# Compressed entries from projected tokens: one 257-column projection, a softmax in 32x32 turned blocks, and x loaded twice

## The chip, the core and the metric

The kernel runs on one NeuronCore of a Trainium2 chip. The metric is device time in microseconds; the time before is the median of three runs, 2910.0 us (2906.97 to 2914.53). All work is in float32 unless said otherwise. A core has a matrix engine (TensorE, PE in the profile, with PEld for its weight loads), three engines for elementwise work (VectorE = DVE, ScalarE = ACT, GpSimd = POOL), and SyncE (SP), whose queue issues most transfers here. A float32 matrix product appears in the trace as two passes, so a product over four blocks of the inner dimension gives eight.

## The reference, cut to what matters

```python
xn = layernorm(x)                                   # x: (4, 1024, 512)
# one compressed entry for every 4 tokens
w_cmp   = softmax((xn @ Wcmp + bcmp).reshape(B, 256, 4))
entries = einsum('bcr,bcrh->bch', w_cmp, xn.reshape(B, 256, 4, 512))
ck = rope(rmsnorm(entries @ Wk + bk, kn_w), block_ends)
cv = entries @ Wv + bv
# 16 heads of 128: the 8 best entries of each query, and a local window of 128
q  = rope(rmsnorm(heads(xn @ Wq + bq), qn_w))
lk = rope(rmsnorm(heads(xn @ Wlk + blk), kn_w));  lv = heads(xn @ Wlv + blv)
merged = 0.5 * (top8_attention(q, ck, cv) + window_attention(q, lk, lv))
out = x + merged @ Wo + bo + fp8_rounded(xn) @ fp8_rounded(input2)
```

The change concerns the lines from `w_cmp` to `cv`, and where `x` comes from in the last line.

## The kernel before, in words

The 4 x 1024 tokens are 32 chunks of 128 tokens, `t = 0..31`, eight chunks to a batch row, `c = t % 8`. A chunk has eight units `u = 0..7` of two heads each, so there are 256 units. One loop over `s = -2..257` writes all engines' programs in order by hand; each engine then runs its own instructions strictly in that order, waiting on semaphores. At step `s` it issues, among others: the scores of unit `s` (`scores`, L532), the context of unit `s - 2`, the top-8 and softmax work of unit `s` (`weigh`, `settle`), the projections of queries and keys of unit `s + 2` (`queries`, L432: eight passes L437 and one bias product L438), the output product of unit `s - 2` (`to_output`, L700: four passes L707), the turning of the probabilities (`turn`, `fetch`: VectorE transposes 32x32 blocks, SyncE stores them to DRAM as `pr` and reads them back as `probT`), the local values of unit `s + 1` (`values_of`, eight passes L506), normalization and rotation of unit `s + 2`, and its transposed keys, again through DRAM (`turn_keys`, `fetch_keys`: `qk` stored, `qT` and `lkT` read).

Work that is done once a chunk stands in two generators that the loop advances twice in every step, by its two calls of `steps()`: a first half A, between `queries` and `to_output`, and a second half B, between `to_output` and `turn`. `yield "A3"` closes the first half of the generator's fourth step, and so on.

- `chunk_prep(t + 2)` is started at unit 6 of chunk `t`. It normalizes the chunk (A0 to A1), transposes it on TensorE (`xp`, A2) to `xnT`, computes the logits as one row on one partition (`lp`, A3: `Wcmp` columns stationary, `xnT` moving), takes the softmax over groups of four on that row (B3 and A4), spreads the weights over 128 partitions by a product with ones (`wp`, A5), multiplies `xnT` by them and sums fours on VectorE (`prod`, `entT`, B5), projects the 32 entries to `ck` and `cv` (`ep`, A6, with the bias as a bfloat16 product), copies both out of PSUM on ScalarE, normalizes and rotates `ck`, and transposes it into `ckT` (`cp`, A9 and B9). It takes ten steps, the last at unit 7 of chunk `t + 1`.
- `chunk_eight(t)`, started at unit 3, rounds the chunk to fp8, multiplies by `input2` (`fp`), and adds the result to the loaded `x` tile, the residual. `to_output` of unit 7 adds the attention's output and stores the tile.

The PSUM tiles of the generators and of `values_of` come from one ring of two (`pp`); the larger VectorE scratch tiles from a ring of three (`scratch`). `x` tiles come from a ring of three. In the first two steps, `s = -2` and `-1`, `until(first, ...)` drives the generator of chunk 0 ahead, while chunk 1's runs at the normal pace from `s = -2` on. The weights of the first three units are loaded on SyncE's queue before the loop, later ones on ScalarE's queue inside it.

Of the kernel before, what the change touches and what calls it, by code (L numbers as in the profile page):

```python
# [12 lines left out]
F32 = mybir.dt.float32  # L13
BF16 = mybir.dt.bfloat16
# [24 lines left out]
def kernel(  # L39
# [57 lines left out]
    def load_x(t):  # L97
        b, c = divmod(t, NCH)
        xt = work.tile([P, HID], F32, tag="x", name=f"x_{t}", bufs=3)
        nc.sync.dma_start(xt, hidden[b, ts(c, P), :])  # L100
        x_tiles[t] = xt
# [17 lines left out]
    def load_wqk(u, engine):  # L119
        for i, w in enumerate((Wq, Wlk)):  # L120
            engine.dma_start(
                wqk_sb[u][:, :, ts(i, 256)], w[:, ts(u, 256)].rearrange("(k p) n -> p k n", p=P)
            )
# [7 lines left out]
    load_x(0)  # L131
    load_wqk(0, nc.sync)
    load_x(1)
    load_angles(0)
    load_wlv(0, nc.sync)
    wkv_sb = const.tile([P, KK, 2 * D], F32, name="wkv_sb")
    nc.sync.dma_start(wkv_sb[:, :, 0:D], Wk.rearrange("(k p) n -> p k n", p=P))
    nc.sync.dma_start(wkv_sb[:, :, D : 2 * D], Wv.rearrange("(k p) n -> p k n", p=P))
    load_wqk(1, nc.sync)
# [8 lines left out]
    wcmp_sb = const.tile([P, KK], F32, name="wcmp_sb")  # L148
    with nc.allow_non_contiguous_dma(reason="512 words once"):
        nc.scalar.dma_start(wcmp_sb, Wcmp.rearrange("(k p) o -> p (k o)", p=P))  # L150
    nc.scalar.dma_start(bias_f[0:NU, 0:256], bq.rearrange("(u n) -> u n", u=NU))
    nc.scalar.dma_start(bias_f[0:NU, 256:512], blk.rearrange("(u n) -> u n", u=NU))
    nc.scalar.dma_start(bias_f[NU : NU + 1, 0:D], bk.partition_broadcast(1))
    nc.scalar.dma_start(bias_f[NU : NU + 1, D : 2 * D], bv.partition_broadcast(1))
# [5 lines left out]
    bcmp_sb = const.tile([1, 1], F32, name="bcmp_sb")  # L160
    nc.scalar.dma_start(bcmp_sb, bcmp.partition_broadcast(1))
# [7 lines left out]
    ones = const.tile([1, P], F32, name="ones")  # L169
    nc.vector.memset(ones, 1.0)  # L170
# [6 lines left out]
    sel = const.tile([P, NU + 1], BF16, name="sel")  # L177
# [4 lines left out]
    def small_constants():  # L182
        nc.vector.tensor_scalar(
            norm_w[:, 0, :], norm_w[:, 0, :], 1.0 / math.sqrt(D), None, ALU.mult
        )

        part = work.tile([P, 1024], F32, tag="probB", name="part", bufs=1).bitcast(BF16)
        part = part[0:BLK, 0:512]
        nc.vector.tensor_copy(bias_b[0:BLK, :], bias_f)
        nc.vector.tensor_tensor(bias_f, bias_f, bias_b[0:BLK, :], ALU.subtract)  # L190
        nc.vector.tensor_copy(part, bias_f)
        nc.vector.tensor_copy(bias_b[BLK : 2 * BLK, :], part)
        nc.vector.tensor_tensor(bias_f, bias_f, part, ALU.subtract)
        nc.vector.tensor_copy(bias_b[2 * BLK : 3 * BLK, :], bias_f)

        nc.vector.tensor_tensor(
            sel, ident[:, 0 : NU + 1], ident[:, BLK : BLK + NU + 1], ALU.add
        )
        nc.vector.tensor_tensor(
            sel, sel, ident[:, 2 * BLK : 2 * BLK + NU + 1], ALU.add  # L200
        )

# [92 lines left out]
    def chunk_prep(t):  # L295

        b, c = divmod(t, NCH)
        xt = x_tiles[t]
# [28 lines left out]
        lp = pp(f"lp_{t}")  # L327
        for k in range(KK):
            nc.tensor.matmul(  # L329
                lp[0:1, 0:P],  # L330
                wcmp_sb[:, k : k + 1],
                xnT[:, k, :],
                start=(k == 0),
                stop=(k == KK - 1),
            )
        yield "A3"
        wlf = work.tile([P, P], F32, tag="few", name=f"wl_{t}", bufs=1)[0:1, :]
        wl = wlf.rearrange("p (n r) -> p n r", r=RATIO)
        red = work.tile([1, 2, NE], F32, tag="red", name=f"red_{t}", bufs=1)
        nc.vector.tensor_scalar(wlf, lp[0:1, 0:P], bcmp_sb[0:1, 0:1], None, ALU.add)  # L340
        nc.vector.tensor_reduce(red[:, 0, :], wl, AX.X, ALU.max)

        def over_r(v):
            return v.unsqueeze(2).to_broadcast([1, NE, RATIO])

        nc.vector.tensor_tensor(wl, wl, over_r(red[:, 0, :]), ALU.subtract)
        nc.scalar.activation(wlf, wlf, AF.Exp)
        yield "B3"
        nc.vector.tensor_reduce(red[:, 1, :], wl, AX.X, ALU.add)
        nc.vector.reciprocal(red[:, 1, :], red[:, 1, :])  # L350
        nc.vector.tensor_tensor(wl, wl, over_r(red[:, 1, :]), ALU.mult)
        yield "A4"
        yield "B4"
        wp = pp(f"wp_{t}")
        nc.tensor.matmul(wp[:, 0:P], ones, wlf, start=True, stop=True)
        yield "A5"
        prod = scratch(f"prod_{t}", (P, KK, P))
        nc.vector.tensor_tensor(
            prod, xnT, wp[:, 0:P].unsqueeze(1).to_broadcast([P, KK, P]), ALU.mult
        )  # L360
        entT = work.tile([P, KK, NE], F32, tag="entT", name=f"entT_{t}", bufs=1)
        nc.vector.tensor_reduce(
            entT.rearrange("p k n -> p (k n)"),
            prod.rearrange("p k (n r) -> p (k n) r", r=RATIO),
            AX.X,
# [3 lines left out]
        ep = pp(f"ep_{t}")  # L369
        for k in range(KK):  # L370
            nc.tensor.matmul(  # L371
                ep[0:NE, 0 : 2 * D],
                entT[:, k, :],
                wkv_sb[:, k, :],
                start=(k == 0),
                stop=False,
            )
        nc.tensor.matmul(
            ep[0:NE, 0 : 2 * D],
            sel[:, NU : NU + 1].to_broadcast([P, NE]),  # L380
            bias_b[:, 0 : 2 * D],
            start=False,
            stop=True,
        )
        yield "A6"
        yield "B6"
        g, o = divmod(c * NE, P)
        nc.scalar.copy(cv[o : o + NE, g, :], ep[0:NE, D : 2 * D])
        ess = work.tile([NE, 1], F32, tag="ess", name=f"ess_{t}", bufs=1)
        square_sum(ess, ep[0:NE, 0:D], f"e{t}")  # L390
        er = rstd_of(ess, 1, 1.0 / D, EPS_RMS, f"er_{t}")
        ck = work.tile([NE, 1, D], F32, tag="ck", name=f"ck_{t}", bufs=1)
        nc.scalar.copy(ck[:, 0, :], ep[0:NE, 0:D])
        yield "A7"
        yield "B7"
# [3 lines left out]
        ra = work.tile([P, P], F32, tag="few", name=f"ra_e{t}", bufs=1)[0:NE, 0:ROPE]  # L399
        rotate(ck, angles[t][1], 1, ra, f"e{t}")  # L400
        yield "A8"
        yield "B8"
        cp = pp(f"cp_{t}")
        nc.tensor.transpose(cp[:, 0:NE], ck[:, 0, :], ident[:NE, :NE])
        yield "A9"
        nc.vector.tensor_copy(ckT[:, ts(c, NE)], cp[:, 0:NE])
        yield "B9"

    def chunk_eight(t):

        xt, xnT = x_tiles[t], chunks[t]
# [288 lines left out]
    def to_output(n):  # L700
# [13 lines left out]
        if u == NU - 1:  # L714
            xt = x_tiles[t]
            nc.vector.tensor_tensor(xt, xt, op, ALU.add)
            nc.sync.dma_start(out[b, ts(c, P), :], xt)
# [24 lines left out]
    small_constants()  # L742
    until(first, "B3")
    masks()

    for s in range(-2, NN + 2):
        t, u = place(s)

        if u == 6 and t + 2 < NT:
            running = [*running[-2:], chunk_prep(t + 2)]  # L750
        if u == 3 and 0 <= t < NT:
            running = [*running[-2:], chunk_eight(t)]
        if u == 3 and 0 <= t and t + 2 < NT:
            load_x(t + 2)
# [6 lines left out]
        if s < 0:  # L761
            until(first, "B5" if s == -2 else "B7")
# [7 lines left out]
        if s == -1:  # L770
            until(first, "B8")
        for_unit(s + 1, (values_of,))
        if s == -1:
            until(first, "B9")
# [72 lines left out]
```

## Time and profile before

| | |
|---|---|
| median of 3 runs | 2910.0 us (2906.97 to 2914.53) |
| the profiled execution | 2908.4 us, its span 2906.6 us |
| granted TensorE clock, mean | 0.995 |
| lp (L329), 256 passes of 128 columns | 33.9 us busy |
| wp (L355), 64 passes of 128 columns | 15.5 us busy |
| ep (L371), 256 passes of 256 columns, with bias (L378) | 61.2 + 8.7 us busy |
| values (L506), 2048 passes of 256 columns, for comparison | 484.0 us busy |
| prod and its sum on VectorE (L358, L362), 32 each | 21.8 + 21.9 us busy |
| six operations on the one-row logits on VectorE (L340 to L351) | 56.7 us busy |
| x loads on SyncE's queue | 32 of 256 KB, 3.1 us from issue to landing |

"Busy" adds up the time in which an instruction of the group runs on its engine, overlaps counted once. A matmul's recorded end is modelled; consecutive passes overlap in the record, and the distance from one start to the next is what a pass takes of the engine. In the timeline a row gives start, length, engine, line and operation, output from inputs, shape, and how many instructions were merged into it.

### The profile page before, as it was taken

The page shows a single profiled execution, that of the slowest core. Times are in us where ns is not written, and L with a number is a line of the kernel's source. Part 1 is how long each engine was busy: PE and PEld are TensorE (multiplying, and loading weights), DVE is VectorE, ACT ScalarE, POOL GpSimd, SP SyncE. Part 2 cuts the span into 40 slices and gives each one's busy share as a digit, 9 for nine tenths or more (in the row PEclk, how much of TensorE's full clock was granted, in tenths as well). Part 3 has the DMA queues.
Part 4 walks back from the last instruction along what each step waited for, and adds up shares of the span by engine and source line. Part 5 has one row for each costly group of instructions (what it writes and reads, how often), then busy time and mean ns, then how long its engine had stood idle before and what let it go on. Part 6 is the DMA issues. An engine that isn't in the chain of part 4 may idle for free.

```text
span 2906.6 us, 49295 instructions
## 1 busy us (share of the span) xinstructions
PE 2855.3 (98%) x13705; PEld 1899.8 (65%) x13705; DVE 2224.0 (77%) x8636; ACT 1291.5 (44%) x5059; POOL 815.1 (28%) x1126
## 2 busy tenths in 40 slices
PE   5999999999999999999999999999999999999998
PEld 3566666666666666766666666666666666666666
DVE  5777777878777777788877777787887777877776
ACT  2444444444444444444444444444444444444443
POOL 3422222222233222222222332222322323222221
PEclk8999999999999999999999999999999999999999
DMA  8544445554444445454444444554454444455444
GB/s 242 162 129 132 130 134 141 145 146 140 128 115 131 127 130 140 143 144 140 142 126 119 127 130 126 146 148 137 141 143 117 128 124 126 126 146 149 139 142 120
DMA packets 634825, 399.86 MB, mean 138 GB/s; under 512 B 315796, under 2 KB 591030, under 8 KB 634550
## 3 DMA queue, kind: packets, MB, share of 16 engines
q1 hardware_dynamic: 622560, 383.18, 47.2%
q10 hardware_dynamic: 11990, 13.53, 1.5%
q8 instruction: 109, 1.79, 0.3%
q14 instruction: 166, 1.36, 0.2%
HBM read 208.30 MB, written 188.22 MB: 136 GB/s over the span
## 4 chain that ended last, share of the span: by engine, by line
PE 93%; DMA 3%; DVE 1%; SPq 1%; issue 0%; ACT 0%; POOL 0%; ACTq 0%; DVEq 0%; POOLq 0%
PE qp L437 30%; PE op L707 15%; PE vp L506 14%; PE cp L674 13%; PE sc L552 5%; PE sc L549 4%; PE sc L542 4%; PE ep L371 2%; PE qp L438 2%; PE sc L540 2%; DMA lkT<-qk 1%; PE lp L329 1%; PE fp L417 1%; DMA qk<-thb 1%; PE xp L319 0%
## 5 line engine op out<-in xcount | busy, mean ns | idle before, releaser
L437 PE MATMUL qp<-wqk,xnT 128*128 128x512 f32 x2048 | 947.1, 605 | 0.2 <-DMA wqk<-in_L_attn_Wlk_dram 0.2
L437 PEld LDWEIGHTS qp<-wqk,xnT 128*128 128x128 f32 x2048 | 371.3, 191 | 381.2 <-issue 371.0
L579 ACT ACTIVATE prob<-sc,neg 128x256 f32<-128x256 f32 (+1 forms) x512 | 235.6, 460 | 649.8 <-DVE taken L578 639.3
L707 PE MATMUL op<-wo,cT 128*128 128x512 f32 x1024 | 494.4, 605 | 1.0 <-ACT cT L689 1.0
L506 PEld LDWEIGHTS vp<-wlv,xnT 128*128 128x128 f32 x2048 | 388.9, 190 | 161.2 <-issue 103.1
L506 PE MATMUL vp<-wlv,xnT 128*128 128x256 f32 x2048 | 484.0, 379 | 0.0
L623 DVE STREAM_TRANSPOSE probB<-prob 128x512 f32<-128x512 f32 (+2 forms) x510 | 288.7, 603 | 161.1 <-ACT prob L605 157.8
L273 ACT ACTIVATE junk<-qp 128x128 bf16<-128x128 f32 x1024 | 283.6, 277 | 236.5 <-PE qp L438 200.8
L267 POOL TENSOR_SCALAR r<-ss 128x4 f32<-128x4 f32 x256 | 49.8, 194 | 1093.5 <-ACT junk L273 1088.1
L518 ACT COPY lv<-vp 128x256 f32<-128x256 f32 x256 | 95.1, 372 | 537.3 <-PE cp L674 455.1
L286 POOL TENSOR_TENSOR rb<-th,cs 128x256 f32<-128x256 f32 x256 | 247.1, 965 | 286.8 <-DVE th L459 286.8
L459 DVE SCALAR_TENSOR_TENSOR th<-qp,r,norm_w 128x128 f32<-128x128 f32 x1024 | 283.1, 337 | 40.1 <-POOL r L268 40.1
L674 PE MATMUL cp<-probT,lv 128*128 128x128 f32 x1920 | 297.7, 275 | 5.8 <-DMA qk<-thb 3.1
L707 PEld LDWEIGHTS op<-wo,cT 128*128 128x128 f32 x1024 | 181.7, 189 | 174.3 <-issue 96.6
L674 PEld LDWEIGHTS cp<-probT,lv 128*128 128x128 f32 x1920 | 274.8, 191 | 21.1 <-issue 3.6
L268 POOL TENSOR_TENSOR r<-r,nhalf 128x4 f32<-128x4 f32 x256 | 259.7, 1014 | 21.3
L674 PE MATMUL cp<-probT,cv 128*128 128x128 f32 x1536 | 255.2, 275 | 0.0
L574 DVE TENSOR_REDUCE neg<-sc 128x1 f32<-128x256 f32 (+1 forms) x512 | 198.3, 387 | 52.8 <-PE sc L553 52.8
L549 PE MATMUL sc<-lkT,qT 128*128 128x128 f32 x1024 | 210.6, 288 | 27.3 <-DMA lkT<-qk 27.1
L552 PE MATMUL sc<-ckT,qT 128*128 128x96 f32 (+7 forms) x1024 | 226.9, 303 | 0.0
L605 ACT ACTIVATE prob<-prob,tot 128x256 f32<-128x256 f32 (+1 forms) x512 | 222.6, 483 | 3.6 <-DVE tot L599 3.6
L674 PEld LDWEIGHTS cp<-probT,cv 128*128 128x128 f32 x1536 | 212.7, 192 | 0.0
(121 smaller groups left out, 4073.5 us busy)
## 6 DMA issues: line engine op xcount, KB each, us to landing
qk<-thb SPq DMA_DIRECT2D x1024, 64.0 KB, 2.0
pr<-probB SPq DMA_DIRECT2D x127, 512.0 KB, 2.6
probT<-pr SPq DMA_DIRECT2D x508, 128.0 KB, 2.9
pr<-probB SPq DMA_DIRECT2D x96, 384.0 KB, 2.3
probT<-pr SPq DMA_DIRECT2D x384, 96.0 KB, 2.4
qT<-qk SPq DMA_DIRECT2D x256, 128.0 KB, 2.3
lkT<-qk SPq DMA_DIRECT2D x256, 128.0 KB, 2.5
x<-_attn_hidden_states_dram SPq DMA_DIRECT2D x32, 256.0 KB, 3.1
```

The source lines that it names most:

```text
L268: nc.gpsimd.tensor_tensor(r, r, nhalf[: ss.shape[0], 0:n], ALU.pow)
L273: nc.scalar.activation(junk[: src.shape[0]], src, AF.Square, accum_out=acc)
L286: nc.gpsimd.tensor_tensor(bb, x12, wide(cs[:, HALF:ROPE]), ALU.mult)
L437: nc.tensor.matmul(qp, xnT[:, k, :], wqk_sb[u][:, k, :], start=(k == 0), stop=False)
L459: nc.vector.scalar_tensor_tensor(th[:, i, :], qp[:, ts(i, D)], r[:, i : i + 1], norm_w[:, i // 2, :], ALU.mult, ALU.mult,)
L506: nc.tensor.matmul(vp[:, 0:256], xnT[:, k, :], wlv_sb[u][:, k, :], start=(k == 0), stop=(k == KK - 1),)
L549: nc.tensor.matmul(blocks(sc[:, P : 2 * P]), q, lkT[:, :, ds(h * BLK, BLK)], start=False, stop=True)
L552: nc.tensor.matmul(sc[:, spa], q, ckT[:, 0:m], start=True, stop=False)
L579: nc.scalar.activation(prob[:, loc], sc[:, loc], AF.Exp, bias=neg[:, 0:1], accum_out=tot[:, 0:1])
L623: nc.vector.transpose(pb[:, :, ds(h * g, g), :], prob[:, parts[0] * P : (parts[-1] + 1) * P].rearrange("p (g b i) -> p b g i", b=NB, i=BLK),)
L674: nc.tensor.matmul(blocks(cp[:, h, :]), v, probT[:, :, h * len(parts) + i - parts[0], :], start=(i == parts[0]), stop=(i == parts[-1]),)
L707: nc.tensor.matmul(op, cT[:, h, :], wo_sb[u][:, h, :], start=(u == 0 and h == 0), stop=(u == NU - 1 and h == 1),)
```

## The change

The entries are a weighted sum over four tokens and the projection is linear, so the order of the two can be exchanged. After the change the chunk's 128 tokens are projected first, with `Wcmp` as a 257th column beside `Wk` and `Wv`, and the weighted sum of fours is taken over projected tokens by a second product with a 128x32 matrix of unnormalized weights. The normalizing sum comes out of the same product, from a column of ones.

- The logits are now a column over 128 partitions. VectorE turns them in 32x32 blocks into a row of each block (`transpose`), takes maximum and difference over fours there, ScalarE the exponential, and VectorE turns them back.
- `picks`, a 0/1 matrix made once on GpSimd, places each token's weight in its entry's column (`spread_w`).
- The bias is added by VectorE from a broadcast tile after the division by the sum; the bias product and the row of `sel` for it are gone.
- `chunk_prep` is one step shorter and starts at unit 7 instead of unit 6; the `until` targets of chunk 0 are renamed accordingly. The last step still falls on unit 7 of the next chunk.
- `x` is loaded twice for each chunk: "norm" for `chunk_prep`, at unit 4 two chunks ahead (before: unit 3), and "sum" for the residual, at unit 3 of the chunk itself. The ring is two tiles instead of three.
- `Wcmp` is loaded on SyncE's queue behind `Wk` and `Wv` instead of at the head of ScalarE's queue; the biases `bk`, `bv` and `bcmp` are broadcast over 32 and 128 partitions.

```diff
-    def load_x(t):
-        xt = work.tile([P, HID], F32, tag="x", name=f"x_{t}", bufs=3)
+    def load_x(t, purpose):
+        xt = work.tile([P, HID], F32, tag="x", name=f"x_{purpose}_{t}")
...
+    wkv_sb = const.tile([P, KK, 2 * D + 1], F32, name="wkv_sb")
     nc.sync.dma_start(wkv_sb[:, :, 0:D], Wk.rearrange("(k p) n -> p k n", p=P))
     nc.sync.dma_start(wkv_sb[:, :, D : 2 * D], Wv.rearrange("(k p) n -> p k n", p=P))
+        nc.sync.dma_start(
+            wkv_sb[:, :, 2 * D : 2 * D + 1], Wcmp.rearrange("(k p) o -> p k o", p=P)
+        )
...
+    def pick_tokens():
+        nc.gpsimd.memset(picks, 1.0)
+        for base, step, mult in ((0, -RATIO, 1), (RATIO - 1, RATIO, -1)):
+            nc.gpsimd.affine_select(out=picks, in_=picks, compare_op=ALU.is_ge, fill=0.0,
+                base=base, pattern=[[step, NE]], channel_multiplier=mult)
...
-        lp = pp(f"lp_{t}")
+        yp = pp(f"yp_{t}")
         for k in range(KK):
             nc.tensor.matmul(
-                lp[0:1, 0:P],
-                wcmp_sb[:, k : k + 1],
+                yp[:, 0 : 2 * D + 1],
                 xnT[:, k, :],
+                wkv_sb[:, k, :],
...
         yield "A3"
...
+        y = scratch(f"y_{t}")[:, 0 : 2 * D + 1]
+        nc.scalar.copy(y[:, 0 : 2 * D], yp[:, 0 : 2 * D])
+        nc.gpsimd.memset(y[:, 2 * D : 2 * D + 1], 1.0)
+        nc.vector.tensor_scalar(
+            logits[:, 0:1], yp[:, 2 * D : 2 * D + 1], bcmp_sb, None, ALU.add
+        )
...
+        nc.vector.transpose(row[:, 0, :], logits)
+        fours = row[:, 0, :].rearrange("p (n r) -> p n r", r=RATIO)
+        nc.vector.tensor_reduce(red, fours, AX.X, ALU.max)
+        nc.vector.tensor_tensor(
+            fours, fours, red.unsqueeze(2).to_broadcast([P, BLK // RATIO, RATIO]), ALU.subtract
+        )
+        nc.scalar.activation(row[:, 0, :], row[:, 0, :], AF.Exp)
         yield "B3"
-        nc.vector.tensor_reduce(red[:, 1, :], wl, AX.X, ALU.add)
-        nc.vector.reciprocal(red[:, 1, :], red[:, 1, :])
-        nc.vector.tensor_tensor(wl, wl, over_r(red[:, 1, :]), ALU.mult)
         yield "A4"
+        nc.vector.transpose(row[:, 1, :], row[:, 0, :])
+        nc.vector.tensor_scalar(spread_w, picks, row[:, 1, 0:1], None, ALU.mult)
         yield "B4"
-        wp = pp(f"wp_{t}")
-        nc.tensor.matmul(wp[:, 0:P], ones, wlf, start=True, stop=True)
+        ep = pp(f"ep_{t}")
+        nc.tensor.matmul(ep[0:NE, 0 : 2 * D + 1], spread_w, y, start=True, stop=True)
         yield "A5"
-        nc.vector.tensor_tensor(
-            prod, xnT, wp[:, 0:P].unsqueeze(1).to_broadcast([P, KK, P]), ALU.mult
-        )
...
+        nc.vector.reciprocal(total, ep[0:NE, 2 * D : 2 * D + 1])
+        nc.vector.scalar_tensor_tensor(
+            kv.rearrange("p h d -> p (h d)"), ep[0:NE, 0 : 2 * D], total, bkv_sb,
+            ALU.mult, ALU.add,
+        )
         yield "B5"
-        for k in range(KK):
-            nc.tensor.matmul(ep[0:NE, 0 : 2 * D], entT[:, k, :], wkv_sb[:, k, :], ...)
-        nc.tensor.matmul(ep[0:NE, 0 : 2 * D], sel[:, NU : NU + 1]..., bias_b[:, 0 : 2 * D], ...)
...
-        if u == 6 and t + 2 < NT:
+        if s == -2 or u == 7 and 0 <= t and t + 2 < NT:
             running = [*running[-2:], chunk_prep(t + 2)]
         if u == 3 and 0 <= t < NT:
+            load_x(t, "sum")
             running = [*running[-2:], chunk_eight(t)]
-        if u == 3 and 0 <= t and t + 2 < NT:
-            load_x(t + 2)
+        if u == 4 and 0 <= t and t + 2 < NT:
+            load_x(t + 2, "norm")
...
-            until(first, "B5" if s == -2 else "B7")
+            until(first, "A5" if s == -2 else "B6")
```

## The prediction

> **What bounds the kernel now.** I read the page's busy shares first, then the chain that ended last, then TensorE's timeline inside one chunk in the middle of the run. From the page, TensorE's row of the first part, and from the chain by engine:
>
> ```profile
> PE 2855.3 (98%) x13705; PEld 1899.8 (65%) x13705; DVE 2224.0 (77%) x8636; ACT 1291.5 (44%) x5059; POOL 815.1 (28%) x1126
> PE 93%; DMA 3%; DVE 1%; SPq 1%; issue 0%; ACT 0%; POOL 0%; ACTq 0%; DVEq 0%; POOLq 0%
> ```
>
> The ends of matmuls are modelled, so 98% alone proves little. The starts are better. Below is TensorE's timeline, four stretches that each begin with the bias matmul L438 closing a unit's queries (first column: start in us):
>
> ```profile
> 1402.17 0.38 PE L438 MATMUL qp<-bias_b,sel 128*128 128x512 bf16 x1
> 1402.48 1.03 PE L329 MATMUL lp<-xnT,wcmp_sb 128*1 128x128 f32 x8
> 1403.44 1.98 PE L707 MATMUL op<-wo,cT 128*128 128x512 f32 x4
> 1405.27 1.89 PE L506 MATMUL vp<-wlv,xnT 128*128 128x256 f32 x8
> 1406.99 0.61 PE L674 MATMUL cp<-probT,lv 128*128 128x128 f32 x4
> ...
> 1414.39 0.38 PE L438 MATMUL qp<-bias_b,sel 128*128 128x512 bf16 x1
> 1414.61 1.88 PE L707 MATMUL op<-wo,cT 128*128 128x512 f32 x4
> 1416.32 1.89 PE L506 MATMUL vp<-wlv,xnT 128*128 128x256 f32 x8
> ...
> 1425.44 0.38 PE L438 MATMUL qp<-bias_b,sel 128*128 128x512 bf16 x1
> 1425.75 0.48 PE L355 MATMUL wp<-wl,ones 1*128 1x128 f32 x2
> 1427.99 1.89 PE L506 MATMUL vp<-wlv,xnT 128*128 128x256 f32 x8
> ...
> 1437.11 0.38 PE L438 MATMUL qp<-bias_b,sel 128*128 128x512 bf16 x1
> 1437.42 1.91 PE L371 MATMUL ep<-wkv_sb,entT 128*32 128x256 f32 x8
> 1439.17 0.27 PE L378 MATMUL ep<-bias_b,sel 128*32 128x256 bf16 x1
> 1439.37 1.98 PE L707 MATMUL op<-wo,cT 128*128 128x512 f32 x4
> 1441.19 1.89 PE L506 MATMUL vp<-wlv,xnT 128*128 128x256 f32 x8
> ```
>
> Each group starts where the one before stops streaming; the values group takes 1405.27 to 1406.99 = 1.72 us for 8 passes, 0.215 each. In the table of stages TensorE is idle 36.5 of the first 120 us, 2.0 of the 85 us around the second batch's first chunk (757 to 842), and 0.7 of the 637 us from 120 to 757. So between 120 and 2850 us a TensorE microsecond removed is a microsecond of the kernel, until another engine takes over.
>
> **A rule that speaks against this.** The Trainium skill (Perfetto Trace Analysis, Identifying the Most-Contended Engine) calls matmul occupancy a poor measure of the distance to roofline and would use weight-load busy share instead. Here that is 65%, so by it TensorE has a third in hand. Counting only weight loads by their rows: gone are 8 x 84 ns (lp), 2 x 182 (wp), 8 x 109 + 97 (ep), 2.00 us a chunk; new are 8 x 190 (as L506) and 2 x 109, 1.74; 0.27 us a chunk, 8 us in all. By the starts it is 1.45 us a chunk, as follows. I take the starts: the gaps that the weight loads leave are where a 512-wide pass streams 0.43 us over a 0.19 us load, not room for anything.
>
> **TensorE, per chunk.** A unit without chunk work takes 1414.39 to 1416.32 = 1.93 us from L438 to L506. With lp it takes 3.10, with wp 2.55, with ep and its bias 4.08. Removed: 1.17 + 0.62 + 2.15 = **3.94 us**. This is more than the streaming: entering a group whose stationary operand is not a full 128x128 costs 0.09 (L438 lasts 0.31 rather than 0.22), leaving it 0.09, and the first pass of L707 behind it is 0.10 longer (1.82 rather than 1.71 for four).
>
> Added, yp: eight passes with xnT as full stationary operand over 257 columns. The nearest row is L506, same stationary tile, 256 columns: 8 x (0.215 + 0.001) = **1.73**. No edge cost, as L506 shows none. Added, the new ep: two passes of 257 columns with a 128x32 stationary operand. Streaming as in L371, 2 x 0.22 = 0.44; with the edges that L371 and L378 show, 0.09 in, 0.09 out, 0.10 on L707, it is 0.72. I take 0.75 (one pass in eight of L371 starts 0.02 late) and keep 0.44 as the lower end. Net 3.94 - 1.73 - 0.75 = **1.46 us a chunk less**; the transposes xp and cp stay, a unit later or in the same unit. Chunks 2 to 31 are prepared at full load: 30 x 1.45 = **-43.5 us**. Chunk 1 is prepared while TensorE still waits for transfers: half of it, -0.7.
>
> **The other engines, steady part.** VectorE loses prod and its reduce (680 + 686), and six one-row operations (332 + 274 + 279 + 267 + 341 + 281): 3.14 us. It gains a 128x1 add (about 0.15, as L577), two 128x32 transposes (L623's widths 256, 384, 512 take 420, 554, 686, so about 0.18 each), a reduce, a subtract and a scaling of 32 columns (0.12 to 0.25 each), a reciprocal (0.17) and a 32x256 multiply-add (about 0.45, between L459 and L422): some 1.65. It is off the path (77%), so 1.5 us less is worth nothing by itself. ScalarE swaps the ck copy (238) for the y copy (as L518, 372); GpSimd gains a 128x1 memset (0.1). Both hidden: 44% and 28% busy.
>
> New waits: the logits add on VectorE and the y copy on ScalarE wait for yp in unit 2; behind them stand turn's transposes, then the pr store, then key loads. The timeline has scores starting at 0 and L438 at 5.3, so yp is ready near 7.4. VectorE finishes settle near 7.0 and turn cannot start before ScalarE's window scaling ends at 8.2. The five small operations last about 0.8, so turn slips 0 to 0.3 us. In unit 3 turn is now behind two short operations rather than 1.37 us of prod and reduce, in unit 4 it gets 0.6 us that fits before 8.2. The ep matmul waits for spread_w, y and the memset, all made a half unit (5 us) or more earlier.
>
> **SyncE's queue.** Each chunk issues one more 256 KB load: "sum" at unit 3, where x was loaded before, "norm" at unit 4, about 0.45 us of issue each and 8.4 MB on 400. Its buffers are free: the store of the previous "sum" is issued in unit 1, two units ahead. Behind the loads stand pr, probT, qk and the key loads. Comparing lkT's issue with the scores that read it gives 2.3 to 3.3 us in unit 3, 3 to 4.4 in unit 4, and 4 to 6 in units 5 and 6 (median landing 2.5); keys issued in unit 4 are for unit 6. So unit 3 is the tight one, because the output store of unit 1 holds SyncE for 2.3 us until op is done. The change loosens it: in unit 1 xp (0.44) stands where lp (1.17) stood, the logits' VectorE chain (0.89) no longer sits between the store and turn, and unit 2 gains 1.73 us of TensorE. The 6 us of key waits at the second, third and fourth batches' first chunks partly go, but units of 9.1 us leave SyncE's own serial chain (pr landing, probT, qk landing, keys: some 9.2 us) as a limit, so part of the 3 x 1.45 us gained there is lost. Net -1, between -5 and +5.
>
> **The start.** Timeline, first 40 us:
>
> ```profile
> 9.74 0.51 SPq L138 DMA_DIRECT2D wkv_sb<-in_L_attn_Wv_dram  x1
> 10.75 1.86 PE L329 MATMUL lp<-xnT,wcmp_sb 128*1 128x128 f32 x8 [2.82 <-ACT xnT L322]
> 12.54 5.08 PE L437 MATMUL qp<-wqk,xnT 128*128 128x512 f32 x8
> 38.23 0.80 PE L549 MATMUL sc<-lkT,qT 128*128 128x128 f32 x2 [9.13 <-DMA lkT<-qk]
> ```
>
> Before, only Wcmp was needed at 10.75; wkv came later. Now yp needs all of it: Wv is issued at 9.74 and lands in 5.5 us, and Wcmp's 512 words queue behind it, so yp starts near 16.5, with a clock that has gone slow (L437 in this stretch ran 1.01 us a pass before 0.43). Behind it stands queries(0): 20 to 23.6 rather than 12.5 to 17.5. The first normalization, at 22.86 before behind VectorE's entry work, comes near 26.8. That is 4 us on the chain to lkT, of which the emptier DMA queues give some back: **+3.5**, from 0 (the keys' transfer was bound by the weights' backlog) to +8. The moved Wcmp issue itself delays the second unit's weights by about 0.5 us, not needed until 18.4.
>
> **Sum.** The profiled execution took 2908.4 us around a span of 2906.6. 2908.4 - 43.5 - 0.7 + 3.5 - 1 = 2866.7. The runs' median is 1.6 above that execution: **2868 us**.
>
> **Rivals.**
> 1. *The columns of odd length cost.* Rows of 257 words start off any round address, and no row of this trace has an odd width. The Trainium skill (SBUF — State Buffer, Door 1: The DMA port swizzle) gives SBUF 16-byte lines that stream at full rate with two hits or more a line, and PSUM 8-byte ones; by it 257 contiguous words cost one extra line, nothing. If every pass went at half rate instead, 10 x 0.217 = 2.17 us a chunk would outweigh 1.45: 2908.4 + 32 x 0.72 + 3.5 = **2935, slower**. It decides from 0.15 us a pass. For it: nothing measured excludes it. Against: L552's widths 96 to 256 go linearly with columns. 8% for slower as a whole.
> 2. *Another wait takes over*: the unit 2 slip and the two loads delay keys by 0.5 to 1 us a chunk beyond the slack of units 4 and 5. 30 x 0.75 = 22 us given back: **2890** (2880 to 2899). For it: unit 4's slack is only some 1 us over the landing. Against: TensorE's own 1.73 us in unit 2 falls in the same stretch. 13%.
> 3. *TensorE has headroom, as the weight-load share says*: 2908.4 - 8 + 3.5, some **2904**, no change. Against: 0.7 us idle in 637. 5%.
>
> The forecast itself: 74%, own range 2857 to 2880 (ep at 0.44 would give 9 less, the start 3.5 less to 4.5 more, the key waits 4 either way). To hold 8 in 10 with half of rival 2: **2856 to 2886**. A measurement tells 0.3%, 8.7 us, from no change. Faster 74 + 13 = 87%, same 5%, slower 8%.
>
> **What would show it.** yp passes 0.216 apart; L438 to values 3.66 us in unit 2, 1.93 in unit 3, some 2.68 in unit 4; TensorE still idle under 1 us per 600; yp first at about 16.5, first keys read near 41. Wrong would be: passes over 0.3 us, TensorE waiting for lkT in units 4 to 6, or a start later by over 8 us.

## The result, and the profile after

| | before | after |
|---|---|---|
| median | 2910.99 us (2906.97 to 2914.53, 4 runs) | 2864.86 us (2862.24 to 2872.34, 4 runs) |
| profiled execution, its span | 2908.4, 2906.6 us | 2864.4, 2862.7 us |
| first scores of unit 8 | 135.5 us | 136.0 us |
| from there to the first scores of unit 248 (30 chunks) | 2674.9 us | 2629.8 us |
| mean granted TensorE clock | 0.995 | 0.995 |

The ratio is 0.9846 with a 95% interval of 0.9823 to 0.9869. The two lower time rows come from the starts of TensorE's instructions in the trace: a unit begins where its first score pass starts, and "the steady part" below always means unit 8 to unit 248.

From the page of the changed kernel, the busy times and the chain that ended last by engine:

```profile
PE 2812.8 (98%) x13417; PEld 1903.9 (67%) x13417; DVE 2209.7 (77%) x8636; ACT 1300.8 (45%) x5059; POOL 816.8 (29%) x1161
PE 21%; DMA 1%; DVE 0%; SPq 0%; ACT 0%; issue 0%; POOL 0%; ACTq 0%
```

TensorE issues 288 passes fewer and is busy 42.5 us less; the weight loads take 4 us more. The chain's shares add up to some 22%: in this execution it could be followed over less than a quarter of the span, and there nearly all of it is TensorE. The table of stages speaks for the rest (window, its length, busy time of TensorE, its weight loads, VectorE, ScalarE and GpSimd with counts, granted clock, DMA share, GB/s):

```profile
0.00:120.00 120.00, 81.36 (x307) 50.54 (x308) 70.67 (x283) 33.97 (x149) 47.21 (x73) 0.89 0.73 218
120.00:757.00 637.00, 636.23 (x3057) 432.25 (x3056) 501.01 (x1929) 295.27 (x1136) 178.14 (x253) 1.00 0.50 142
757.00:842.00 85.00, 84.36 (x389) 54.68 (x388) 61.83 (x291) 38.33 (x166) 26.21 (x38) 1.00 0.45 122
```

TensorE idles 0.8 of the 637 us, as before. In the 85 us around the second batch's first chunk it idles 0.6 where it idled 2.0.

TensorE's timeline inside a chunk answers to the stretches shown before (columns: start, length, engine, line, operation, output from inputs, stationary shape, moving shape, passes):

```profile
1393.40 0.38 PE L443 MATMUL qp<-bias_b,sel 128*128 128x512 bf16 x1
1393.61 1.90 PE L349 MATMUL yp<-wkv_sb,xnT 128*128 128x257 f32 x8
1395.35 1.88 PE L712 MATMUL op<-wo,cT 128*128 128x512 f32 x4
1397.07 1.89 PE L511 MATMUL vp<-wlv,xnT 128*128 128x256 f32 x8
...
1406.19 0.38 PE L443 MATMUL qp<-bias_b,sel 128*128 128x512 bf16 x1
1406.41 1.88 PE L712 MATMUL op<-wo,cT 128*128 128x512 f32 x4
...
1417.25 0.38 PE L443 MATMUL qp<-bias_b,sel 128*128 128x512 bf16 x1
1417.56 0.62 PE L379 MATMUL ep<-y,spread 128*32 128x257 f32 x2
1418.11 1.98 PE L712 MATMUL op<-wo,cT 128*128 128x512 f32 x4
1419.93 1.89 PE L511 MATMUL vp<-wlv,xnT 128*128 128x256 f32 x8
```

From the query bias to the values, unit 2 takes 1393.40 to 1397.07 = 3.67 us, and unit 4 takes 1417.25 to 1419.93 = 2.68. Group `yp` has no edge: `op` starts 1.74 us after it and takes its usual 1.72. Group `ep` shows all three edges: 0.31 instead of 0.22 before it, 0.55 for two passes of 0.22, and 1.82 instead of 1.71 for the four passes behind it. Where neither kernel waits for keys, as in chunks 5, 13 and 21, a chunk takes 90.90 us from first scores to first scores instead of 92.33: **1.43 us less**. Thirty of these are 42.9 of the 45.1 us that the steady part lost.

The start, as the timeline has it (in brackets the idle time before and what ended it):

```profile
9.73 0.51 SPq L140 DMA_DIRECT2D wkv_sb<-in_L_attn_Wv_dram  x1
10.28 0.51 SPq L142 DMA_DIRECT2D wkv_sb<-in_L_attn_Wcmp_dram  x1
15.41 3.76 PE L349 MATMUL yp<-wkv_sb,xnT 128*128 128x257 f32 x8 [8.00 <-DMA wkv_sb<-in_L_attn_Wcmp_dram]
26.03 1.13 DVE L464 SCALAR_TENSOR_TENSOR th<-qp,r,norm_w 128x128 f32<-128x128 f32 x4 [3.90 <-POOL r L288]
33.16 0.51 SPq L503 DMA_DIRECT2D lkT<-qk  x1
36.64 0.76 PE L554 MATMUL sc<-lkT,qT 128*128 128x128 f32 x2 [1.58 <-DMA lkT<-qk]
```

and the load of the first keys in the kernel before:

```profile
30.82 0.51 SPq L498 DMA_DIRECT2D lkT<-qk  x1
```

TensorE's first product now stands until `Wcmp` has landed, 4.7 us later than before, and the first normalization comes 3.2 us later. The first keys, however, are read at 36.64 us, 1.6 us earlier than before: from the issue of `lkT` to the pass that reads it 3.5 us go by here, and 7.4 went by before.

### The profile page after: what moved, and what is told of

The parts are those of the page before. It is cut to its first block, busy times and chain, and to the rows that moved or that the text cites. A ratio compares the mean times of both kernels' runs of the same rounds, so it can differ in the third digit from the quotient of the medians.

```text
span 2862.7 us, 48785 instructions
## 1 busy us (share of the span) xinstructions
PE 2812.8 (98%) x13417; PEld 1903.9 (67%) x13417; DVE 2209.7 (77%) x8636; ACT 1300.8 (45%) x5059; POOL 816.8 (29%) x1161
## 5 line engine op out<-in xcount | busy, mean ns | idle before, releaser
L712 PE MATMUL op<-wo,cT 128*128 128x512 f32 x1024 | 488.0, 599 | 0.6 <-ACT cT L694 0.5
L628 DVE STREAM_TRANSPOSE probB<-prob 128x512 f32<-128x512 f32 (+2 forms) x510 | 289.1, 604 | 143.4 <-ACT prob L610 136.2
L464 DVE SCALAR_TENSOR_TENSOR th<-qp,r,norm_w 128x128 f32<-128x128 f32 x1024 | 282.8, 338 | 27.4 <-POOL r L288 26.9
L288 POOL TENSOR_TENSOR r<-r,nhalf 128x4 f32<-128x4 f32 x256 | 259.7, 1014 | 21.4
L308 DVE TENSOR_TENSOR th<-thb,rb 128x128 f32<-128x128 f32 x256 | 87.2, 341 | 158.6 <-POOL rb L306 158.6
```

The lines of the kernel that those rows point to most:

```text
L288: nc.gpsimd.tensor_tensor(r, r, nhalf[: ss.shape[0], 0:n], ALU.pow)
L464: nc.vector.scalar_tensor_tensor(th[:, i, :], qp[:, ts(i, D)], r[:, i : i + 1], norm_w[:, i // 2, :], ALU.mult, ALU.mult,)
L628: nc.vector.transpose(pb[:, :, ds(h * g, g), :], prob[:, parts[0] * P : (parts[-1] + 1) * P].rearrange("p (g b i) -> p b g i", b=NB, i=BLK),)
L712: nc.tensor.matmul(op, cT[:, h, :], wo_sb[u][:, h, :], start=(u == 0 and h == 0), stop=(u == NU - 1 and h == 1),)
```

## Experiments

Each run has, beside its median, two readings of its trace that need no total: the length of the steady part, and the **key waits** in it, the time by which passes on `lkT` started later than the usual distance behind the pass before (each by over 0.1 us, between 145 and 2750 us; the usual distance is the median of the run).

| run | median us | ratio to before, 95% | unit 8 at | steady part | key waits |
|---|---|---|---|---|---|
| before | 2910.99 | 1 | 135.5 | 2674.9 | 7.7 |
| after | 2864.86 | 0.9846 [0.9823, 0.9869] | 136.0 | 2629.8 | 6.1 |
| after, taken again | 2869.30 | 0.9851 [0.9837, 0.9864] | 140.1 | 2630.0 | 4.4 |
| yp twice | 2921.74 | 1.0037 [1.0026, 1.0048] | 145.4 | 2678.6 | 2.8 |
| prod and sum put back | 2867.38 | 0.9844 [0.9828, 0.9861] | 136.9 | 2634.4 | 7.3 |
| x loaded once | 2866.12 | 0.9845 [0.983, 0.986] | 139.3 | 2628.0 | 3.8 |
| store behind the keys | 2867.09 | 0.9851 [0.9838, 0.9865] | 140.8 | 2630.7 | 4.1 |
| projection weights first | 2857.64 | 0.9822 [0.9809, 0.9836] | 131.4 | 2628.3 | 4.0 |
| ep padded | 2861.72 | 0.9828 [0.9814, 0.9843] | 143.4 | 2624.1 | 8.7 |
| ep and cp padded | 2850.55 | 0.9793 [0.9779, 0.9806] | 135.1 | 2618.7 | 12.0 |
| both padded, store behind | 2852.59 | 0.9806 [0.9793, 0.982] | 136.5 | 2617.2 | 10.6 |
| both padded, weights first | 2847.37 | 0.9776 [0.9762, 0.979] | 132.2 | 2617.2 | 9.7 |
| spread_w on ScalarE | 2866.02 | 0.9842 [0.9828, 0.9855] | 136.5 | 2629.9 | 5.8 |
| both padded, weights first, spread_w on ScalarE | 2843.60 | 0.9767 [0.9753, 0.978] | 132.7 | 2612.4 | 5.6 |

**Is TensorE the bound at the margin?** The eight passes of `yp` are issued twice into the same tile.

```diff
-        for k in range(KK):
+        for k in [*range(KK), *range(KK)]:
```

> The changed kernel with yp's eight passes issued twice (the second overwrites the first, same output). Theory (TensorE's streaming is the bound): 8 x 0.217 = 1.73 us a chunk come back, 30 chunks at full load 52 us, and some 3 to 5 more at the start: 2917 to 2922. Rival (the gain came from VectorE, SyncE's queue or the keys' slack, TensorE has headroom): 2865 to 2875.

The timeline has the doubled group in unit 2:

```profile
1426.02 3.64 PE L349 MATMUL yp<-wkv_sb,xnT 128*128 128x257 f32 x16
1429.50 1.88 PE L712 MATMUL op<-wo,cT 128*128 128x512 f32 x4
```

Sixteen passes take 3.48 us, 0.2175 each, and the kernel 57 us more than the changed one: 32 times 1.74 is 55.7. The steady part grew by 48.8 us where 30 times 1.74 are 52.2; the key waits fell by 3.3 in the longer units, which is the difference. A TensorE microsecond added is a microsecond of the kernel, less what it hides of the key waits, so the third that the weight-load share seems to leave isn't there. It also shows the price of the odd width: in the trace of the changed kernel from 145 us on, passes of 257 columns stand 0.2178 us apart, those of 256 columns 0.2158.

**Does the work taken off VectorE matter?** The product and sum over fours come back with no reader.

```diff
+        prod = scratch(f"prod_{t}", (P, KK, P))
+        nc.vector.tensor_tensor(prod, xnT, xnT, ALU.mult)
+        entT = work.tile([P, KK, NE], F32, tag="entT", name=f"entT_{t}", bufs=1)
+        nc.vector.tensor_reduce(...)
```

> The changed kernel with a product and a sum of fours of the size of the old prod and entT put back on VectorE at the same place (behind the entry product, results unused): 1.37 us of VectorE a chunk, 44 us in all. Theory (VectorE is off the path): 2863 to 2869. Rival (VectorE's shorter chain made the gain): 2895 to 2909.

VectorE's busy time rose to 2245.4 us, and the ratio is that of the change within 0.0002. In the steady part this one profile is 4.6 us longer. Of that 1.2 are key waits, and up to 1.7 are a stretch of 3.4 us at half the clock (0.57 granted on the mean from 822 to 826 us, where both profiles of the changed kernel have 1.00). So the work taken off VectorE bought a few microseconds at most and nothing that the total shows.

**Does the second load of x cost?** The residual takes the tile that the normalization read, and the ring is three tiles again; some small tiles share memory to make room for the third.

```diff
-        xt = work.tile([P, HID], F32, tag="x", name=f"x_{purpose}_{t}")
+        xt = work.tile([P, HID], F32, tag="x", name=f"x_{purpose}_{t}", bufs=3)
...
-            xt = x_tiles.pop(("sum", t))
+            xt = x_tiles.pop(("norm", t))
...
-            load_x(t, "sum")
```

> The changed kernel with x loaded once, at unit 4 two chunks ahead, in a ring of three that the residual reads too; three small tiles share the row tile's space so that the third x tile fits. Theory (the second load is hidden in SyncE's slack): no change, 2860 to 2868. Rival (the extra 32 loads of 256 KB cost key waits): 5 to 15 us less, 2850 to 2860.

No difference in the total. The steady part is 1.8 us shorter and the key waits are 2.3 smaller, but the changed kernel's own two profiles differ by 1.7 in the latter. The 8.4 MB more are hidden, and SyncE's extra issue costs 2 us at most.

**Does SyncE's hold on the output store cost?** The store of unit 7 is issued behind the key loads of the step rather than ahead of the turn.

```diff
-            nc.sync.dma_start(out[b, ts(c, P), :], xt)
+            stores.append((out[b, ts(c, P), :], xt))
...
+        while stores:
+            nc.sync.dma_start(*stores.pop())
```

> The changed kernel with the output store issued at the end of its step, behind the key loads, instead of ahead of the turned probabilities. Theory (TensorE is the bound, SyncE's hold in unit 1 is hidden since the change): the hold of some 2 us on SyncE goes and the key waits between 120 and 2800 us (about 6 us) fall by at most 4: 2861 to 2865. Rival (SyncE's hold in unit 1 still costs a wait in each chunk): 15 to 30 us less, 2835 to 2850.

No change: the rival that SyncE's hold costs something in every chunk fell. The few microseconds that the theory allowed (2861 to 2865) did not come either.

**What does the start cost?** The loads of `Wk`, `Wv` and `Wcmp` are moved directly behind the first x load, ahead of the query and value weights.

```diff
+    nc.sync.dma_start(wkv_sb[:, :, 0:D], Wk.rearrange("(k p) n -> p k n", p=P))
...
     load_wqk(0, nc.sync)
     load_x(1, "norm")
     load_angles(0)
     load_wlv(0, nc.sync)
-    nc.sync.dma_start(wkv_sb[:, :, 0:D], Wk.rearrange("(k p) n -> p k n", p=P))
...
```

> The changed kernel with Wk, Wv and Wcmp loaded right behind the first x tile, ahead of the first unit's query and key weights. Theory (yp waits at the start for Wcmp behind 3 MB of weights): yp starts near 10 us rather than 15.4, the first queries end near 18 rather than 23, and the chain to the first keys is up to 4 us shorter: 2861 to 2865, seen in the trace of the start rather than in the total. Rival (the start is bound by the weights' traffic and not by yp): first keys read as late as before, 2863 to 2868.

`yp` starts at 9.26 us instead of 15.41, the first normalization at 20.69 instead of 26.03, the first keys are read at 33.11 instead of 36.64. Unit 8 begins 4.6 us earlier than in one profile of the changed kernel and 8.7 than in the other, and the median is 7.2 below it, more than was expected. So the wait of the first product for the whole of `wkv_sb` was a real cost. How large it is depends on which profile of the changed kernel it is held against, as the next run shows.

**How much does the same kernel differ from itself?** The changed kernel once more, with nothing edited, in a later session.

> The changed kernel as it is, a second profile beside the two variants before: the steady part from unit 8 to unit 248 within 3 us of the first profile's 2629.8 us if the variants' differences there are the variants' own; the first eight units may differ by several us if the start varies from one execution to the next (profiles of kernels with the same start gave 136 to 143 us for unit 8).

The steady part agrees within 0.2 us, and the first 40 us within 0.3 (`yp` at 15.17, first keys read at 36.53). Between units 5 and 6 of chunk 0, however, this execution took 5.7 us longer, of which 4.1 were left at unit 8: unit 5 begins at 103.9 in both, unit 6 at 115.8 and 121.5. The traces show what the time went into. TensorE's waits for keys between 100 and 125 us (us, times, longest), and the stretch from 108 to 115 us in the table of stages (granted clock third from the end), first of the first profile and then of the second:

```profile
PE sc L554 <- DMA lkT<-qk: 2.7, 2, 1.7
108.00:115.00 7.00, 7.00 (x24) 3.81 (x24) 6.29 (x33) 3.22 (x16) 2.43 (x4) 1.00 0.35 96
```

```profile
PE sc L554 <- DMA lkT<-qk: 4.4, 1, 4.4
108.00:115.00 7.00, 6.54 (x17) 3.98 (x18) 4.52 (x27) 1.27 (x6) 0.31 (x1) 0.51 0.40 116
```

The keys of unit 5 came 2.6 us later, and towards the end of that wait, at 108.1 us, the clock fell to half for 6.8 us: the scores and queries behind it take 3.1 us longer, the query passes standing up to 1.0 us apart instead of 0.43. The profiles with the doubled `yp`, the store behind the keys and `ep` padded, whose unit 8 is latest, have both in the same place, a wait of 4.1 to 4.8 us and 6.8 us of half clock; with `x` loaded once there is a shorter stretch a unit later (3.4 us), and in the remaining ones there is none between unit 5 and unit 8. That the wait brings the slow clock on was not tested. The kernels that share this start (all but those with the weights first and the doubled `yp`) have unit 8 between 135.1 and 143.4. So the start's cost, read from one profile each, is known to some 5 us and no better; the medians carry this spread as well.

**Can the edges be had back?** `picks` and `spread_w` are made 128 columns wide with zeros beyond the 32 entries, so that the stationary operand of `ep` is a full 128x128.

```diff
-    picks = const.tile([P, NE], F32, name="picks")
+    picks = const.tile([P, P], F32, name="picks")
...
-        spread_w = work.tile([P, NE], F32, tag="spread", name=f"spread_{t}", bufs=1)
+        spread_w = work.tile([P, P], F32, tag="spread", name=f"spread_{t}", bufs=1)
...
-        nc.tensor.matmul(ep[0:NE, 0 : 2 * D + 1], spread_w, y, start=True, stop=True)
+        nc.tensor.matmul(ep[:, 0 : 2 * D + 1], spread_w, y, start=True, stop=True)
```

> The changed kernel with ep's stationary operand widened from 32 to 128 columns, the others zero: same streaming, more weights. Theory (a stationary operand that is not a full 128x128 costs 0.09 us on entry, 0.09 on leaving and 0.10 on the next group's first pass): 30 x 0.29 = 8.7 us less, about 2856, L443 before ep lasting 0.22 rather than 0.31. Rival (the edges come from short groups or from the semaphore waits of these groups): no change, or 1 to 3 us more for the wider scaling and weight load: 2864 to 2868.

Its TensorE timeline in a unit 4:

```profile
1420.85 0.60 PE L380 MATMUL ep<-y,spread 128*128 128x257 f32 x2
1421.29 1.88 PE L713 MATMUL op<-wo,cT 128*128 128x512 f32 x4
1423.00 1.24 PE L512 MATMUL vp<-wlv,xnT 128*128 128x256 f32 x5
```

Two passes now take 0.44 us instead of 0.55, and the four behind them 1.71 instead of 1.82; the 0.09 ahead of the group is gone too. From its first query pass to the values unit 4 takes 5.88 us instead of 6.20 (6.197 and 5.883). That is 0.31 a chunk, 9.4 us over the steady part, of which 5.7 arrived: the key waits rose by 2.6. The total, 3 us less, lies between what the theory and the rival expected and is within the spread of the start, so it is the steady part that decides for the theory.

The transpose of the keys of the entries has the same edges, and was padded in the next run together with `ep` (a zeroed tile of 128 rows holds the 32 entries).

```diff
-        nc.tensor.transpose(cp[:, 0:NE], ck[:, 0, :], ident[:NE, :NE])
+        nc.tensor.transpose(cp[:, 0:P], kv_sb[:, 0, :], ident)
```

> e5_ep_full with the entry keys' transpose also given a full 128x128 stationary operand (a kv tile of 128 partitions, zero below the entries, one pass of 128 columns instead of 32). Theory: its edges go too, 0.22 instead of 0.31 on entry, 0.11 instead of 0.17 for the pass, 0.10 less on the next group: 0.26 us a chunk, 30 x 0.26 = 8 us below e5_ep_full in the steady part, total 2851 to 2856 where key waits don't take it. Rival (only ep's edges came from its stationary operand): as e5_ep_full, 2859 to 2864.

The changed kernel's timeline at the transpose, in unit 7:

```profile
1452.03 0.38 PE L443 MATMUL qp<-bias_b,sel 128*128 128x512 bf16 x1
1452.34 0.24 PE L409 MATMUL cp<-ident,kv 32*128 32x32 f32 x1
1452.51 1.98 PE L712 MATMUL op<-wo,cT 128*128 128x512 f32 x4
1454.33 1.89 PE L511 MATMUL vp<-wlv,xnT 128*128 128x256 f32 x8
```

and that of the padded one:

```profile
1445.93 0.27 PE L412 MATMUL cp<-ident,kv_sb 128*128 128x128 f32 x1
1446.04 1.88 PE L715 MATMUL op<-wo,cT 128*128 128x512 f32 x4
1447.76 1.89 PE L514 MATMUL vp<-wlv,xnT 128*128 128x256 f32 x8
```

A transpose of four times as many columns out of four times as many rows takes 0.11 us of TensorE instead of 0.17 and takes the edges with it: 1.99 us from the transpose to the values become 1.83, and the 0.09 ahead goes as well. The kernel gains 14 us on the changed one. Of the 0.57 us a chunk that the two paddings free (0.31 and 0.26), 17.2 in all, the steady part shows 11.1; the key waits rose by 5.9, to 12.0, which is the rest.

Next came the kernel with both paddings and, as in the run above, the store issued behind the keys:

> e6_ep_cp_full and e8_store_late together. Theory (the full operands save 0.55 us of TensorE a chunk, and what they lost went to key waits behind SyncE's queue): 2846 to 2853. Rival (the two do not add up because another wait takes over): 2855 to 2862.

Neither time nor key waits moved beyond the spread (12.0 to 10.6): the store isn't what holds the keys.

Then both paddings with the loads of `wkv_sb` moved up front, as above:

> e6_ep_cp_full with the loads ordered as in e4_wkv_first. Theory (TensorE's edges in the steady part and the late Wcmp at the start are separate costs): the gains add, 14 + 7 us below the changed kernel, 2842 to 2847. Rival (both are the same slack counted twice): as e6_ep_cp_full, 2849 to 2853.

Padding and the earlier weights add up: 2847.4, 22 us below the changed kernel in the same session.

**What holds the keys, then?** In the kernels with both paddings most of the waits stand in unit 5, whose keys are fetched in unit 3. There the profile of the changed kernel has this, on VectorE, ScalarE, GpSimd and SyncE's queue:

```profile
1408.07 0.20 DVE L375 STREAM_TRANSPOSE row<-row 128x32 f32<-128x32 f32 x1
1408.13 0.90 ACT L610 ACTIVATE prob<-prob,tot 128x256 f32<-128x256 f32 x2
1408.30 1.27 POOL L265 TENSOR_TENSOR qv_x<-qv_x,qm_x 128x512 f32<-128x512 f32 x1 [7.59 <-DVE row L375]
1408.31 1.30 DVE L376 TENSOR_SCALAR spread<-picks,row 128x32 f32<-128x32 f32 x1
1409.52 1.29 DVE L628 STREAM_TRANSPOSE probB<-prob 128x512 f32<-128x512 f32 x2
1410.84 0.34 SPq L636 DMA_DIRECT2D pr<-probB  x1
1410.98 0.35 DVE L464 SCALAR_TENSOR_TENSOR th<-qp,r,norm_w 128x128 f32<-128x128 f32 x1 [0.17 <-POOL r L288]
```

A product over 32 columns lasts 1.30 us, as long as GpSimd's addition over 512 columns that starts 0.01 us ahead of it. In the first chunk, where GpSimd is idle, the same instruction takes 0.24:

```profile
21.07 0.24 DVE L376 TENSOR_SCALAR spread<-picks,row 128x32 f32<-128x32 f32 x1
```

In the second it takes 0.24 too, and in the other 30, all of them beside that addition, 1.23 to 1.30 (the expectation below counts one more). The Trainium skill (SBUF — State Buffer, Who interferes with whom) says that VectorE shares its second pair of ports with GpSimd, that a `tensor_scalar` between SBUF tiles can take it, and that the one which issues first keeps the pair for its whole instruction while the other stands. For the addition the numbers here agree: it starts 0.01 to 0.08 us before the product and ends 0.04 before it. Not every GpSimd instruction does this, however: in the second chunk the power over four columns (L288) runs from 0.29 us before the product to 0.50 behind it, and the product isn't held. Behind the product stands the turn, and behind the turn `pr` and the keys. The product was moved to ScalarE:

```diff
-        nc.vector.tensor_scalar(spread_w, picks, row[:, 1, 0:1], None, ALU.mult)
+        nc.scalar.mul(spread_w, picks, row[:, 1, 0:1])
```

> The changed kernel, with the product of picks and the turned weights (spread_w) computed by ScalarE instead of VectorE. In the changed kernel this VectorE product of 32 columns takes 1.30 us in 31 of 32 chunks and 0.24 in the one where GpSimd is idle; each long one ends with GpSimd's 128x512 addition of the rounding, which starts in the same moment. In unit 3 it ends 0.5 us after ScalarE's window scaling, so the turn of the probabilities starts 0.5 us late there, and with it the store of pr and the keys fetched behind it for unit 5. Theory (this holds the keys): the turn in unit 3 starts when ScalarE's window scaling ends; waits for keys in the steady part fall from 4.5 to 6.1 us to under 3, the steady part from 2630 to 2626 to 2628, the median to 2861 to 2866. Rival (the keys are held by the x loads and SyncE's own chain): the turn moves, the waits and the steady part do not (2629.5 to 2630.5), median as the changed kernel (2864 to 2870).

The same place of the new kernel:

```profile
1407.00 0.90 ACT L610 ACTIVATE prob<-prob,tot 128x256 f32<-128x256 f32 x2
1407.16 1.28 POOL L265 TENSOR_TENSOR qv_x<-qv_x,qm_x 128x512 f32<-128x512 f32 x1 [7.60 <-DVE row L375]
1407.53 1.30 DVE L628 STREAM_TRANSPOSE probB<-prob 128x512 f32<-128x512 f32 x2 [0.39 <-ACT prob L610]
1407.80 0.31 ACT L376 ACTIVATE spread<-picks,row 128x32 f32<-128x32 f32 x1
1408.86 0.34 SPq L636 DMA_DIRECT2D pr<-probB  x1
1409.85 0.35 DVE L464 SCALAR_TENSOR_TENSOR th<-qp,r,norm_w 128x128 f32<-128x128 f32 x1 [1.02 <-POOL r L288]
```

From the start of the window scaling to the store of `pr`, 2.71 us became 1.86. VectorE's next work, the normalization L464, did not move: it starts 2.7 us after GpSimd's addition in both, since it waits for GpSimd's `r`, which stands behind that addition. But the total didn't move either, and the key waits stayed at 5.8: for the changed kernel as it is, the theory failed. By place it was half right: outside the first chunks of the batches the key waits fell from 3.2 us (2.3 in the second profile) to 0.3, and at the first chunks, where units last down to 9.1 us, they rose from 2.9 (2.1) to 5.5.

The same edit in the kernel with both paddings and the weights first:

> The best kernel so far (both small stationary operands padded, weights of the projection loaded first), with spread_w computed by ScalarE. There the waits for keys are 9.9 us in the steady part, most of them in unit 5. Theory: they fall by 3 to 6 us, the steady part from 2617.2 to 2611 to 2614, the median from 2847 to 2841 to 2845. Rival: the waits stay at 8 to 11, the steady part at 2616.5 to 2618, the median at 2844 to 2850.

In the padded kernel it holds. The key waits fell from 9.7 to 5.6 and the steady part from 2617.2 to 2612.4. Outside the first chunks of batches unit 5 lasts 11.44 us on the mean instead of 11.61, 27 times 0.17 = 4.6 us. The waits of TensorE for keys between 145 and 2750 us, in the view of waits (us, times, longest), first without and then with the product on ScalarE:

```profile
PE sc L557 <- DMA lkT<-qk: 5.9, 7, 1.2
```

```profile
PE sc L557 <- DMA lkT<-qk: 3.2, 4, 1.6
```

The total is 3.8 us lower, at 2843.6, but the intervals of the two ratios overlap, so it is the steady part, in one profile each, that carries this. It is the fastest version tried, 67 us below the kernel before and 21 below the changed one.

## Why the prediction was right, point by point

**TensorE, right to 0.03 us a chunk.** The forecast had 3.94 off, 1.73 and 0.75 on, net 1.46, of which 1.45 went into the sum; the trace shows 1.43. Unit 2 takes 3.67 us (3.66 forecast), unit 4 2.68 (2.68), unit 3 1.93. What carried it was counting starts to starts, edges included: by the streaming alone (0.44 for `ep`) the sum would have been 9 us too hopeful.

**VectorE's entry work, one term mis-sized, without effect on the time.** The scaling of 32 columns was put at 0.12 to 0.25 us and took 1.23 on the mean. So VectorE lost 14.3 us where some 48 were forecast; with the product on ScalarE it is 49.2 (2224.0 to 2174.8). That VectorE's time is worth next to nothing by itself was borne out by the run that put 1.37 us a chunk back. The step that failed is the duration taken from the number of columns alone, without asking what GpSimd does in that moment.

**The slip of the turn, mis-sized.** The forecast was 0 to 0.3 us in unit 2, the logits being ready with `yp`. In the changed kernel's timeline of a unit 2:

```profile
1396.14 0.36 ACT L358 COPY y<-yp 128x256 f32<-128x256 f32 x1
1396.53 0.22 DVE L360 TENSOR_SCALAR logits<-yp,bcmp_sb 128x1 f32<-128x1 f32 x1 [1.97 <-ACT y L358]
1396.78 0.21 DVE L365 STREAM_TRANSPOSE row<-logits 128x32 f32<-128x32 f32 x1
1397.36 1.30 DVE L628 STREAM_TRANSPOSE probB<-prob 128x512 f32<-128x512 f32 x2
```

the logits wait for ScalarE's copy of `y`, which itself comes after the window scaling, and not for `yp`, though the code has both only read `yp`. The turn starts 1.1 us behind the end of that scaling. (The forecast also let the turn wait for the scaling's end; with the product on ScalarE it starts 0.53 us after the scaling begins, when the first head is done.) In unit 3, where the forecast saw only relief, the product beside GpSimd held it by 0.9. Both stayed hidden: the unit is 1.73 us longer by `yp`, and unit 3's delay matters only once TensorE is shorter still.

**SyncE and the keys, right in sign.** Forecast -1 (between -5 and +5); the key waits went from 7.7 to 6.1 and 4.4. They left units 3 and 4 and reappeared, smaller, mostly in units 5 to 7. That unit 3 had been the tight one, and would be loosened, is what the places show; that the output store's hold on SyncE was the reason isn't, since moving the store changed nothing in the changed kernel, and in the kernel before it wasn't tried.

**The start, right in its first half.** `yp` was forecast near 16.5 us and came at 15.4, the first normalization near 26.8 and came at 26.0. The first keys, forecast near 41, came at 36.6, since their transfer took 3.5 us and not 7.4; the forecast had named emptier queues as a gain, but what made it shorter wasn't tried. Of the forecast +3.5 (with -0.7 for chunk 1), one profile shows +0.5 and the other +4.6 at unit 8. The run with the weights first shows that the wait costs 5 to 9 us against a start without it, so it was worth naming. That the total fell within 4 us of the forecast (2864.9, and 2869.3 in the later session, for 2868) owes something to luck: the forecast missed the first keys by 4.4 us, and did not know the spread of the start, which is as large.

**The sum.** Between the two profiled spans: start +0.5, steady part -45.1, end +0.7, together -43.9, where the forecast had -41.7.

**The rivals.** Odd columns cost 0.002 us a pass, not 0.15. A new wait did appear in units 5 to 7, but it was smaller than the one that went. Headroom on TensorE is excluded by the doubled `yp`. So the reading of the weight-load share that the prediction weighed (the Trainium skill, Perfetto Trace Analysis, Identifying the Most-Contended Engine), a third of TensorE in hand at 65%, doesn't hold here. (The page names the share together with MFU, the part of the peak arithmetic that a kernel reaches; that was not worked out.) The count of weight loads behind it, 8 us less, did not come out either: their busy time rose by 4 us.

**What stays open.** Why the keys of unit 5 of the first chunk come 2.6 us later in one execution than in another, whether the half clock there follows from that wait, and what holds the keys in the first chunks of the batches.

## What to carry to other kernels

Where one engine is never idle, price an edit by the distance from start to start in the place where it stands, with the edges of odd-shaped neighbours, and not by busy time or by the share of another resource. Of a moved load, ask which in-order engine has its first instruction waiting for it; of a small instruction put on VectorE, ask what GpSimd runs in the same moment. A small stationary operand can be cheaper padded to a full one with zeros.

## What the runs showed of the hardware that was not expected

- Two groups whose stationary operand wasn't 128x128 (`ep` with 128x32, the transpose `cp` with 32x32) cost 0.09 us ahead and 0.10 in the next group, and `ep` about 0.1 behind its last pass; padded with zeros to 128x128 they cost none of it. The two paddings shortened TensorE's work by 0.57 us a chunk, of 87.7, and the kernel by 14 us.
- One VectorE product of 32 columns took 1.30 us beside a GpSimd addition of 1.27 us over 512 columns, and 0.24 alone or beside a GpSimd power of 1.03 us over four; padded to 128 columns 1.34 and 0.29. On ScalarE at the same moment it took 0.31, undisturbed.
- Two profiles of one kernel agree within 0.2 us over 2630 us of steady work and differ by 4.1 us in the first 140, by a longer wait for keys and a stretch of 6.8 us at half the TensorE clock.
- The shorter TensorE became, the longer it waited for keys: 6.1, 8.7 and 12.0 us with none, one and two paddings, so that a third of what the paddings freed was lost until the product beside GpSimd was moved.
